# Two-layer attention and experts kernel: 72 tiles of layer 0 made always, five behind a branch

## The chip, the core and the metric

The kernel runs on one core of a Trainium2 chip. A core has five engines that work at the same time, each from its own list of instructions: PE (matrix products), DVE (element by element work and reductions), ACT (activations and copies), POOL (element work, and the DMAs whose rows are looked up) and SP (DMAs). They wait for each other on semaphores. The metric is the time of one execution in microseconds (us); lower is better. The kernel before takes 2041.83 us, the median of 6 runs that reach from 2031.76 to 2045.89.

## What is computed

The input x is 8 sequences of 1024 tokens of 128 numbers. Two layers follow each other, each an attention and a set of experts, and each part is added to what came in:

```python
x = x + L0_attention(layernorm(x))   # 8 heads of 32, softmax
x = x + L0_experts(layernorm(x))     # 14 experts, each token goes to 2
x = x + L1_attention(layernorm(x))   # linear attention, 16 heads of 8
x = x + L1_experts(layernorm(x))     # 8 experts, each token goes to 1
```

The experts of layer 0 are what the change is about. A gate gives each token 14 logits; the two largest choose its experts and its two weights w. Each expert is a small network, y = gelu(x W1 + b1) W2 + b2 with 256 hidden numbers, and the token's result is x + w0 y0 + w1 y1. So 2 x 8192 = 16384 pairs of a token and an expert are to be worked, and how many fall to which expert is known only when the kernel runs.

## The kernel before

**Layer 0 attention** (up to about 1310 us of the profiled execution) computes the attention, the gate and the choice of experts. Each token's normalised row is copied by a DMA on POOL (line 582, `rows_in<-xn,at`) into a table in DRAM, `rows_in`, which has a region of 256 + 8192 rows for each expert. The first 256 rows of each region, and a spare tile at the end, are zeroed at the start of the kernel from a tile of zeros, `nil` (issued through the helper at line 207, inside `load_rest`); so that an expert's tiles can be filled up with zeros in front.

**Layer 0 tiles.** The rows of an expert are cut into tiles of 256 (`TW0`). An expert with r rows has r / 256 tiles, rounded up; each of 14 experts can waste less than one tile, so at most 16384 / 256 + 13 = 77 tiles (`NT0`) are needed. The kernel always makes 77. `expert_tables` (lines 117 to 158) works out with a few small DVE operations, for each tile j, which expert it belongs to (`exp_j`) and which row of `rows_in` it starts at (`row_j`); `upto` is the running sum of tiles over the experts, and its last entry the number of tiles that hold a row. Tiles past that number take the last expert's weights and the spare tile of zeros. SP and DVE read six entries of the tables at a time into registers (`looked_up`, line 167).

The loop over j (from line 941) is written out in full, and PE, DVE, ACT and SP keep the order in which it is written; POOL's instructions are placed by a scheduler. For each tile:

- SP fetches 256 rows (line 863, `xr<-rows_in`), four tiles ahead.
- DVE copies the expert's weights from the table `blob` to `wt` (line 871), two tiles ahead.
- PE transposes the rows (line 877, `px`), ACT copies them out (line 879, `xt`).
- PE makes the hidden numbers (line 886, `ph`), ACT applies gelu (line 889, `g`).
- PE makes the output (line 896, `py`), DVE adds b2 and the row itself (lines 901 and 905, `y`).
- POOL writes the tile to the table `rows_out` in DRAM (line 906, `rows_out<-y`).

Between the tiles DVE works out where each token's two results stand in `rows_out` (`found`, in `places`). At j = 8 the loads and constants of layer 1 are issued, and at j = NT0 - 8 an unread gather on POOL (`warm`, line 843), which the scheduler has placed ahead of the first write of a tile.

**Layer 1 attention** begins when `rows_out` is whole. POOL gathers for each 128 tokens the rows of their two experts (line 1054, `got<-rows_out,found`), ACT and DVE weigh and add them (lines 1073 and 1079), and the normalisation, products and so on follow from line 1089. The first gather on POOL waits for all writes of `rows_out`, in a row of separate waits.

**Layer 1 tiles** end the kernel in the same way, and there a branch exists already: 36 tiles are made always, a flag `over` is read into a register of each engine (line 1627) and the rest of the tiles stands behind `tc.If(crowd > 0)` (line 1631), which is passed over in the profiled execution. A branch of this kind has no meeting of all engines. Each engine reads the flag itself, compares and jumps. On the path that skips the work, each engine raises the semaphores that the skipped work would have raised, so that waits further on keep their numbers; on POOL that is an instruction of its own, `INC_SWDGE_SEM`.

Of the kernel before, what the change touches and what calls it, by code (L numbers as in the profile page):

```python
# [12 lines left out]
ALU = mybir.AluOpType  # L13
# [3 lines left out]
P = 128  # L17
NB = 8
T = 1024
D = 128  # L20
# [8 lines left out]
E0, F0 = 14, 256  # L29
K0 = F0 // P  # L30
CAP0 = NB * T
TW0 = 256
TI0 = TW0 // P

NT0 = 2 * NB * T // TW0 + E0 - 1
REG0 = TW0 + CAP0
ROWS0 = E0 * REG0 + TW0

# [22 lines left out]
NT1_MAIN = 36  # L61
ROWS1 = E1 * REG0 + TW0
RW1 = 2 * D + 1
# [8 lines left out]
C_J = C_TW + CAP0 // TW0  # L72
C_TOK = C_J + NT0
C_END = C_TOK + NCHUNK
# [3 lines left out]
def tile_two_layers(  # L78
# [5 lines left out]
    nc = tc.nc  # L84
# [96 lines left out]
    rows_in = dram.tile([ROWS0, D], F32, name="rows_in")  # L181
    rows_out = dram.tile([NT0 * TW0, D], F32, name="rows_out")

# [4 lines left out]
    counts = routes.tile([P, E0], F32, name="counts")  # L188
    nc.gpsimd.memset(counts, 0.0)
    found = routes.tile([P, NB, 2, CPB], U32, name="found")  # L190
    layer0w = ctx.enter_context(ExitStack())
    blob = layer0w.enter_context(tc.tile_pool(name="blob", bufs=1)).tile([P, E0, B_END], F32, name="blob")

    with ExitStack() as ph:
# [11 lines left out]
        def pinned(f, *args, **kw):  # L206
            return tc.keep_in_program_order(f(*args, **kw))  # L207
# [17 lines left out]
        def load_rest():  # L225
            for b in range(1, NB):
                pinned(nc.sync.dma_start, out=xs[b], in_=x[b].rearrange("(c p) d -> p c d", p=P))
            pinned(nc.sync.dma_start, out=blob, in_=blob0)
            nil = work.tile([P, TI0 * D], F32, name="nil", tag="nums", bufs=1)
            pinned(nc.gpsimd.memset, nil, 0.0)  # L230
            pinned(
                nc.gpsimd.dma_start,
                out=rows_in[:E0 * REG0, :].rearrange("(e r) d -> e r d", e=E0)[:, :TW0, :].rearrange(
                    "e (p i) d -> p e (i d)", i=TI0
                ),
                in_=nil.unsqueeze(1).to_broadcast([P, E0, TI0 * D]),
            )
            pinned(
                nc.gpsimd.dma_start,
                out=rows_in[E0 * REG0:, :].rearrange("(p i) d -> p (i d)", i=TI0), in_=nil,  # L240
            )

        vs, outs = {}, {}
# [467 lines left out]
        for n, qb in blocks:  # L711
            for kc in range(CPB):
                for hp in range(2):
# [30 lines left out]
                    if hp == 1:  # L744
                        weighing = (n, qb, kc, e)
                        if kc % 2 == 0:
                            first = e
# [98 lines left out]

    with ExitStack() as ph:
        tab = ph.enter_context(tc.tile_pool(name="b_tab", bufs=1, reuse_waits="tile"))  # L850
        work = ph.enter_context(tc.tile_pool(name="b_work", bufs=2, reuse_waits="tile"))
        px = ph.enter_context(tc.tile_pool(name="b_px", bufs=2, space=PSUM, reuse_waits="tile"))
        ph_ps = ph.enter_context(tc.tile_pool(name="b_ph", bufs=4, space=PSUM, reuse_waits="tile"))
        py_ps = ph.enter_context(tc.tile_pool(name="b_py", bufs=2, space=PSUM, reuse_waits="tile"))

        tables0 = expert_tables(tab, px, "px", counts, E0, NT0)
        row_of = looked_up(tables0.row_j, NT0, mybir.EngineType.SP, E0 * REG0)
        expert_of = looked_up(tables0.exp_j, NT0, mybir.EngineType.DVE, E0 - 1)

        def fetch(j):  # L860
            r = row_of(j)
            t = work.tile([P, TI0, D], F32, name="xr", bufs=6)
            nc.sync.dma_start(
                out=t, in_=rows_in[bass.ds(r, TW0), :].rearrange("(p i) d -> p i d", i=TI0)
            )
            return t

        def stage(j):
            e = expert_of(j)
            t = work.tile([P, 1, B_END], F32, name="wt", bufs=4)  # L870
            nc.vector.tensor_copy(t, blob[:, bass.ds(e, 1), :])
            return t[:, 0, :]

        def turn(t):
            ps = px.tile([P, TI0, P], F32, name="px")
            for i in range(TI0):
                nc.tensor.transpose(ps[:, i, :], t[:, i, :], ident)  # L877
            xt = work.tile([P, TW0], F32, name="xt", bufs=3)
            nc.scalar.copy(xt, ps.rearrange("p i t -> p (i t)"))
            return xt  # L880

        def hidden0(w, xt):
            g = work.tile([P, K0, TW0], F32, name="g", bufs=3)
            for k in range(K0):
                ps = ph_ps.tile([P, TW0], F32, name="ph")
                nc.tensor.matmul(  # L886
                    ps, lhsT=w[:, B_W1 + k * P:B_W1 + (k + 1) * P], rhs=xt, start=True, stop=True
                )
                nc.scalar.activation(g[:, k, :], ps, AF.Gelu, bias=w[:, B_B1 + k:B_B1 + k + 1])
            return g  # L890

        def output0(j, t, w, g):
            ps = py_ps.tile([P, TI0, D], F32, name="py")
            for i in range(TI0):
                for k in range(K0):
                    nc.tensor.matmul(  # L896
                        ps[:, i, :], lhsT=g[:, k, i * P:(i + 1) * P],
                        rhs=w[:, B_W2 + k * D:B_W2 + (k + 1) * D], start=k == 0, stop=k == K0 - 1,
                    )
            y = work.tile([P, TI0, D], F32, name="y", bufs=4)  # L900
            nc.vector.tensor_tensor(
                y, ps, w[:, B_B2:B_B2 + D].unsqueeze(1).to_broadcast([P, TI0, D]), ALU.add
            )

            nc.vector.tensor_tensor(y, y, t, ALU.add)  # L905
            nc.gpsimd.dma_start(  # L906
                out=rows_out[j * TW0:(j + 1) * TW0, :].rearrange("(p i) d -> p i d", i=TI0), in_=y
            )

        def places():  # L910

            half = NB // 2 * CPB
            shape = [P, half, E0]
            for b in range(0, NB, NB // 2):
                for k in range(2):
                    bs = slice(b, b + NB // 2)
                    pick = work.tile(shape, F32, name="pick", bufs=1)
                    of_expert = chosen[:, k, bs, :].rearrange("p b c -> p (b c)").unsqueeze(2).to_broadcast(shape)
                    yield lambda: nc.vector.tensor_tensor(
                        pick, of_expert, cst[:, C_I14:C_I14 + E0].unsqueeze(1).to_broadcast(shape), ALU.is_equal  # L920
                    )
                    yield lambda: nc.vector.tensor_tensor(
                        pick, pick, tables0.base.unsqueeze(1).to_broadcast(shape), ALU.mult
                    )
                    to = work.tile([P, half], F32, name="to", bufs=1)
                    yield lambda: nc.vector.tensor_reduce(to, pick, AX.X, ALU.add)
                    yield lambda: nc.vector.tensor_tensor(
                        found[:, bs, k, :], ranks[:, k, bs, :], to.rearrange("p (b c) -> p b c", b=NB // 2),
                        ALU.subtract,
                    )  # L930

        with tc.manual_schedule(
            engines={
                mybir.EngineType.PE, mybir.EngineType.DVE, mybir.EngineType.Activation, mybir.EngineType.SP
            }
        ):
            placing = places()
            made, ahead = [], [fetch(j) for j in range(4)]
            weights = [stage(j) for j in range(2)]
            t = ahead.pop(0)  # L940
            ready = [(t, turn(t))]
            for j in range(NT0):
                if j + 4 < NT0:
                    ahead.append(fetch(j + 4))
                if j + 2 < NT0:
                    weights.append(stage(j + 2))
                if ahead:
                    t = ahead.pop(0)
                    ready.append((t, turn(t)))
                (t, xt), w = ready.pop(0), weights.pop(0)  # L950
                made.append((j, t, w, hidden0(w, xt)))
                if len(made) > 1:
                    output0(*made.pop(0))
                if j == 8:
                    load_layer1()
                    make_layer1()
                if j == NT0 - 8:
                    warm()
                if j >= 16 and j % 3 == 1:
                    for piece in placing:  # L960
                        piece()
                        break
            output0(*made.pop(0))
            assert next(placing, None) is None
    layer0w.close()


# [8 lines left out]
    with ExitStack() as ph:  # L976
# [504 lines left out]
        p = NPAIR - 1  # L1481
# [15 lines left out]
        first, second = (Route(NB - 1, c0, CPB // 2) for c0 in (0, CPB // 2))  # L1497
# [28 lines left out]
    with ExitStack() as ph:  # L1526
        tab = ph.enter_context(tc.tile_pool(name="d_tab", bufs=1, reuse_waits="tile"))
# [97 lines left out]
        with ExitStack() as main:  # L1625
            tiles1(main, 0, NT1_MAIN)
        crowd = nc.values_load(
            over, min_val=0, max_val=NB * T,
            skip_runtime_bounds_check_because="it is made of counts",
# [199 lines left out]
```

## Time and profile before

| what | value |
|---|---|
| median of 6 runs | 2041.83 us (2031.76 to 2045.89) |
| the profiled execution: time | 2046.37 us |
| the profiled execution: span from first to last instruction | 2044.6 us |
| mean granted clock of PE | 0.955 |
| PE busy | 1936.1 us (95%) |
| DVE, ACT, POOL busy | 1393.2, 1114.7, 1206.0 us |
| layer 0 tiles | from 1322.5 us (first fetch) to 1480.9 us (last write issued) |
| first gather of layer 1 | 1487.0 us |

The page gives busy times by engine, 40 slices of the span, DMA queues, shares of the chain that ended last, and the costliest groups of instructions. Four views of the trace are used beside it: the chain of what ended last in order of time, where each step is followed back to what released it, and "issue" is time in which an engine waited for nothing that is shown; windows, which give the busy time of each engine and the granted clock of PE in stretches of time; the instructions of one line, with the entries of an engine's sequencer marked by a q (POOLq, DVEq); and the timeline. PEld is the loading of weights into PE, which overlaps its products. A tile's name stands to the left of the arrow where it is written and to the right where it is read.

### The profile page before, as it was taken

The numbers are of one execution on the slowest core, as the hardware profiler recorded it, in microseconds if no ns is written. First come the engines' busy times: TensorE is split into PE (matmuls) and PEld (weight loads), VectorE is DVE, ScalarE is ACT, GpSimd is POOL, SyncE is SP. The second block draws the span as 40 slices with busy tenths as digits, with TensorE's granted clock in tenths as the row PEclk, the third lists the DMA queues.
The fourth block names the chain that finished last, engine by engine and source line by source line (L and its number), as shares of the span: only waits on it lengthen the run. The fifth ranks groups of instructions, "written<-read, shape, count | busy, mean of one in ns | idle before, by whom it ended". The sixth has DMA issues, their size and how long they took to land. (4 is left out here: it accounts for less than half of the span.)

```text
span 2044.6 us, 45296 instructions
## 1 busy us (share of the span) xinstructions
PE 1936.1 (95%) x17406; PEld 1003.6 (49%) x17406; DVE 1393.2 (68%) x3565; ACT 1114.7 (55%) x2351; POOL 1206.0 (59%) x1320
## 2 busy tenths in 40 slices
PE   7999999999999999999999997499959999996997
PEld 3333333333333333333333333299837777775897
DVE  6667768768768768768767776566637777775453
ACT  2555665665565565565555454266536666762443
POOL 1456556667667766766766766422255467644465
PEclk9899999999999999999999998699959999996999
DMA  7000000000000000000000000144322211111331
GB/s 228 1 2 2 2 2 3 8 8 8 9 8 8 9 6 9 8 8 9 8 8 8 13 8 26 36 133 135 124 60 74 88 60 54 49 37 62 107 108 58
DMA packets 49807, 81.58 MB, mean 40 GB/s; under 512 B 13369, under 2 KB 32384, under 8 KB 49456
## 3 DMA queue, kind: packets, MB, share of 16 engines
q0 software_dynamic: 17808, 41.55, 6.0%
q1 hardware_dynamic: 28384, 29.10, 4.9%
q10 hardware_dynamic: 3392, 7.95, 1.2%
q8 instruction: 140, 2.29, 0.5%
q14 instruction: 83, 0.68, 0.1%
HBM read 42.73 MB, written 35.96 MB: 38 GB/s over the span
## 5 line engine op out<-in xcount | busy, mean ns | idle before, releaser
L338 DVE TENSOR_REDUCE nmp<-big 128x1 f32<-128x512 f32 x1000 | 642.2, 683 | 289.0 <-PE st L374 245.9
L377 ACT ACTIVATE e<-st 128x512 f32<-128x512 f32 x1000 | 544.5, 595 | 480.8 <-PE st L374 423.6
L207 POOL TENSOR_TENSOR e<-e 128x512 f32<-128x512 f32 x488 | 604.0, 1268 | 53.2 <-PE num L391 52.7
L334 PE MATMUL big<-kT,qT 32*128 32x512 f32 x2000 | 633.2, 645 | 0.2 <-DVE nmp L338 0.2
L374 PE MATMUL st<-qT,kT 32*128 32x512 f32 x2000 | 535.0, 592 | 0.0
L391 PE MATMUL num<-e,v 128*32 128x512 f32 x3064 | 302.7, 469 | 8.5 <-ACT nums L419 8.5
L207 POOL TENSOR_TENSOR outT<-nums,dens 128x64 f32<-128x64 f32 x248 | 80.7, 326 | 353.3 <-DVE dens L409 259.2
L374 PEld LDWEIGHTS st<-qT,kT 32*128 32x128 f32 x2000 | 215.2, 192 | 3.7 <-issue 1.7
L373 PE MATMUL st<-nb,ones_h 3*128 3x512 bf16 x1000 | 212.9, 386 | 1.3 <-DVE nmp L338 1.3
L391 PEld LDWEIGHTS num<-e,v 128*32 128x32 f32 x3064 | 61.2, 108 | 298.3 <-issue 271.3
L334 PEld LDWEIGHTS big<-kT,qT 32*128 32x128 f32 x2000 | 194.7, 184 | 22.0 <-DVE nmp L338 17.3
L373 PEld LDWEIGHTS <-ones_h 3*128 3x128 bf16 x1024 | 51.2, 91 | 314.4 <-issue 307.7
L1054 POOL DMA_INDIRECT got<-rows_out,found x128 | 126.3, 987 | 94.3 <-PE tp L1089 43.3
L582 POOL DMA_INDIRECT rows_in<-xn,at x128 | 131.6, 1028 | 38.5 <-issue 29.6
L409 DVE RECIPROCAL dens<-dens 128x64 f32<-128x64 f32 x248 | 130.2, 537 | 17.5 <-ACT dens L404 17.4
L391 PE MATMUL den<-e,ones 128*32 128x512 f32 x1032 | 140.0, 611 | 0.2 <-POOL e L207 0.2
L1599 POOL DMA_INDIRECT out_x<-y,to x72 | 79.1, 1099 | 68.6 <-DVE y L1597 51.8
L1580 ACT ACTIVATE g<-ph,wt 128x256 f32<-128x256 f32 x144 | 63.9, 475 | 86.7 <-PE ph L1577 86.6
L906 POOL DMA_DIRECT2D rows_out<-y x77 | 44.7, 580 | 107.0 <-DVE y L905 99.8
L1109 ACT ACTIVATE qm<-qk,cst 128x256 f32<-128x256 f32 x128 | 54.6, 496 | 53.9 <-DVE qk L1106 53.9
L896 PEld LDWEIGHTS py<-wt,g 128*128 128x128 f32 x616 | 81.0, 192 | 4.0
L896 PE MATMUL py<-wt,g 128*128 128x128 f32 x616 | 81.1, 275 | 0.0
(284 smaller groups left out, 2938.1 us busy)
## 6 DMA issues: line engine op xcount, KB each, us to landing
xr<-rows_in SPq DMA_DIRECT2D x77, 128.0 KB
rows_out<-y POOLq DMA_DIRECT2D x77, 128.0 KB, 2.3
xr<-rows SPq DMA_DIRECT2D x36, 257.0 KB
nb<-part SPq DMA_DIRECT2D x384, 1.0 KB
blob<-in_blob ACTq DMA_DIRECT2D x8, 578.0 KB
blob<-in_blob SPq DMA_DIRECT2D x1, 4494.0 KB
x<-in_x SPq DMA_DIRECT2D x8, 512.0 KB
rows<-nil ACTq DMA_DIRECT2D x9, 257.0 KB
```

The lines of the kernel that those rows point to most:

```text
L207: return tc.keep_in_program_order(f(*args, **kw))
L334: nc.tensor.matmul(ps, lhsT=qTs[n][r, qc * P:(qc + 1) * P], rhs=kTs[n][r, kb * BLK:(kb + 1) * BLK], start=True, stop=True,)
L338: nc.vector.tensor_reduce(nmps[n][:, h, qc, kb:kb + 1], ps, AX.X, ALU.max, negate=True)
L373: nc.tensor.matmul(st, lhsT=ones_h[r3, :], rhs=nbs[n][r3, cols], start=True, stop=False)
L374: nc.tensor.matmul(st, lhsT=kTs[n][r, kc * P:(kc + 1) * P], rhs=qTs[n][r, cols], start=False, stop=True)
L377: nc.scalar.activation(e[:, h, :], st, AF.Exp, scale=SCALE0)
L391: nc.tensor.matmul(vds[key][32 * h:32 * h + 32, cols], lhsT=ones[:, :HD0] if den else vs[b][:, kc, c0:c0 + HD0], rhs=e[:, h, cols], start= ...
L409: nc.vector.reciprocal(s[:, cols], s[:, cols])
L582: ins = nc.gpsimd.indirect_dma_start(out=rows_in, out_offset=bass.IndirectOffsetOnAxis(ap=ats[k][:, j:j + 1], axis=0), in_=xn[:, c0 + j, : ...
L896: nc.tensor.matmul(ps[:, i, :], lhsT=g[:, k, i * P:(i + 1) * P], rhs=w[:, B_W2 + k * D:B_W2 + (k + 1) * D], start=k == 0, stop=k == K0 - 1,)
L1054: ins = tc.keep_in_program_order(nc.gpsimd.indirect_dma_start(out=gots[p][:, i, k, :], out_offset=None, in_=rows_out, in_offset=bass.Indir ...
L1599: ins = nc.gpsimd.indirect_dma_start(out=out_rows, out_offset=bass.IndirectOffsetOnAxis(ap=at[:, i:i + 1], axis=0), in_=y[:, i, :], in_off ...
```

## The change

The loop over tiles becomes a function, `tiles0(ph, first, last)`, which is called twice: for tiles 0 to 71, and, behind a branch, for tiles 72 to 76. The flag `over0` is the number of tiles that hold a row, less 72, and at least 0; it is made by one DVE operation right behind the tables. The tables are made once, for 77 tiles, and kept in a pool that now outlives the loop. The work that is woven into the loop (`places`, layer 1's loads, `warm`) stays in the first call. The five last tiles' rows of `rows_out` are zeroed at the start of the kernel, by one more DMA on POOL behind the two that zero rows of `rows_in`. In the built program, the bodies behind the branch hold 52 instructions of PE, 32 of DVE, 20 of ACT, 17 of SP and 11 of POOL; the order of all other instructions is as before but for two neighbours in the tables.

```diff
+NT0_MAIN = 72
...
+            pinned(
+                nc.gpsimd.dma_start,
+                out=rows_out[NT0_MAIN * TW0:, :].rearrange("(j p i) d -> p j (i d)", p=P, i=TI0),
+                in_=nil.unsqueeze(1).to_broadcast([P, NT0 - NT0_MAIN, TI0 * D]),
+            )
...
-    with ExitStack() as ph:
-        tab = ph.enter_context(tc.tile_pool(name="b_tab", bufs=1, reuse_waits="tile"))
+    tab0 = layer0w.enter_context(tc.tile_pool(name="b_tab", bufs=1, reuse_waits="tile"))
+    over0 = tab0.tile([1, 1], mybir.dt.int32, name="over0")
+    held0 = SimpleNamespace()
+
+    def tiles0(ph, first, last):
+
         work = ph.enter_context(tc.tile_pool(name="b_work", bufs=2, reuse_waits="tile"))
...
-        tables0 = expert_tables(tab, px, "px", counts, E0, NT0)
+        if first == 0:
+            held0.tables = expert_tables(tab0, px, "px", counts, E0, NT0)
+            nc.vector.tensor_scalar(
+                over0, held0.tables.upto[0:1, E0 - 1:], float(-NT0_MAIN), 0.0, ALU.add, ALU.max
+            )
+        tables0 = held0.tables
...
-            placing = places()
-            made, ahead = [], [fetch(j) for j in range(4)]
-            weights = [stage(j) for j in range(2)]
+            placing = places() if first == 0 else iter(())
+            made, ahead = [], [fetch(j) for j in range(first, min(first + 4, last))]
+            weights = [stage(j) for j in range(first, first + 2)]
             t = ahead.pop(0)
             ready = [(t, turn(t))]
-            for j in range(NT0):
-                if j + 4 < NT0:
+            for j in range(first, last):
+                if j + 4 < last:
                     ahead.append(fetch(j + 4))
-                if j + 2 < NT0:
+                if j + 2 < last:
                     weights.append(stage(j + 2))
...
-                if j == NT0 - 8:
+                if j == NT0_MAIN - 8:
                     warm()
...
+    with ExitStack() as ph:
+        tiles0(ph, 0, NT0_MAIN)
+    crowd0 = nc.values_load(
+        over0, min_val=0, max_val=NT0, skip_runtime_bounds_check_because="it is made of counts",
+    )
+    with tc.If(crowd0 > 0):
+        with ExitStack() as ph:
+            tiles0(ph, NT0_MAIN, NT0)
     layer0w.close()
```

## The prediction

> **What bounds the kernel now.** I read the page first. PE is busy 95% of the span, so a tile of layer 0 that is left out is worth what it costs on PE, if PE sets the pace in that stage. The view of windows says that it does: in seven stretches of 20 us from 1332 to 1472 us PE is busy for 20.00 of 20.00 with the granted clock at 1.00, while DVE is at 13 to 15, ACT at 13 and POOL at 6. Then I read the chain of what ended last, at the end of the tiles. Its columns are start, duration and what ran, in us:
>
> ```profile
> 1472.21 0.89 PE py L896 x8
> 1473.10 0.22 PE px L877 x2
> 1473.32 0.86 PE ph L886 x4
> 1474.19 0.89 PE py L896 x8
> ...
> 1477.92 1.80 PE py L896 x16
> 1479.74 0.44 DVE y L901
> 1480.20 0.44 DVE y L905
> ...
> 1480.92 1.98 DMA rows_out<-y
> ...
> 1483.65 3.30 issue
> 1486.96 1.00 POOL got L1054
> ```
>
> One tile is px, ph and py on PE, and nothing stands between them: the step from py to py is 0.89 + 0.22 + 0.86 = 1.97 us. (From 1331.99 to 1365.56 the same chain has 17 steps, 33.57 / 17 = 1.975 us.) Behind the last tile the chain leaves PE: the last y, its write to rows_out (1.98 us to landing), POOL's waits, 3.30 us in which POOL waits for nothing that is shown, then the first gather of layer 1. PE stands still from 1479.7 to 1498.3. So whatever the branch adds to POOL behind the last write is paid in full; what it adds to the other four engines has some 10 us of cover.
>
> For the price of a branch the kernel has one of its own, at its end, also passed over. The view of lines 1627 (reading the flag) and 1631 (the branch) gives each engine's sequencer; the columns are count, least/median/greatest duration in ns, and the first and last start in us:
>
> ```profile
> L1627 POOLq TENSOR_LOAD <-over x1: 498/498/498, 2033.0 to 2033.0; - x1
> ...
> L1631 POOLq EVENT_SEMAPHORE  x4: 17/43/43, 2036.4 to 2037.3; - x4
> L1631 DVEq EVENT_SEMAPHORE  x2: 21/21/21, 2035.4 to 2035.5; - x2
> ...
> L1631 ACTq COMPARE_BRANCH  x1: 58/58/58, 2028.5 to 2028.5; - x1
> L1631 ACTq EVENT_SEMAPHORE  x1: 17/17/17, 2029.0 to 2029.0; - x1
> L1631 PEldq COMPARE_BRANCH  x1: 3615/3615/3615, 2029.9 to 2029.9; - x1
> L1631 DVEq COMPARE_BRANCH  x1: 72/72/72, 2032.4 to 2032.4; - x1
> L1631 POOLq COMPARE_BRANCH  x1: 53/53/53, 2033.6 to 2033.6; - x1
> ...
> L1631 POOLq INC_SWDGE_SEM  x1: 1380/1380/1380, 2037.4 to 2037.4; - x1
> ```
>
> The reader is to see how far each engine jumps. By the built program the skipped body there holds 100 instructions of ACT, 295 of DVE, 246 of POOL and 482 of PE. ACT is past its jump 0.5 us after the branch began (2028.5 to 2029.0). DVE needs 3.0 us, POOL 2.8, and PE's branch itself 3.6. A short jump is cheap, a long one costs about 3 us.
>
> **The change, part by part.**
>
> *Tiles left out.* Whether the branch is passed over depends on the data. The reference's own routing on its inputs gives the 14 experts 1020 to 1447 rows (1020, 1119, 1116, 1288, 1304, 1077, 1447, 1061, 1116, 1063, 1138, 1369, 1012, 1254); rounded up to tiles of 256 that is 4+5+5+6+6+5+6+5+5+5+5+6+4+5 = 72. The flag is max(72 - 72, 0) = 0, so the five tiles are skipped. Per tile go 8 matmuls and their weight loads, a copy of weights and two adds on DVE, 3 instructions on ACT, a fetch on SP and a write on POOL. By the chain only PE's counts: 5 x 1.975 = **9.9 us saved**. The fill and drain of the tile pipeline are the same as before, one stage earlier.
>
> *Zeroing five tiles of rows_out.* One more write on POOL at about 12.3 us, 5 x 128 KB. The same write of 14 tiles takes POOL 1.33 us and that of one 0.61, so this takes about 0.8 us; POOL next has work at 59.9 us. The 0.66 MB on the DMA engines are some 1.9 us at the 352 GB/s of the window 30 to 35 us. All loads are through by 35 us (the window 35 to 40 shows 5 GB/s), and SP's next transfers leave at 44.2. Cost 0. Without that cover it would be 1.9 us.
>
> *The flag.* One small DVE operation in the tables (their neighbours of this kind take 0.15 to 0.24 us), and the lists of instructions show no other move than two neighbours changing places. row_j is ready at 1319.8; reading it takes SP 0.5 to 1.5 us, so 1321.3 at the latest, and the first fetch leaves at 1322.5, behind the scatter into rows_in that lands at 1322.3. Cost 0 with about 1 us of cover, 0.2 us without.
>
> *The branch on PE, ACT, DVE and SP.* Reading the flag (0.28 to 0.49 us) and jumping over 52, 20, 32 and 17 instructions, all shorter than ACT's 100. ACT and DVE next work on the first gather, nearly 10 us after their last tile, PE at 1498.3. Cost 0; even a jump of 3.6 us would be covered.
>
> *The branch on POOL.* Here all is on the path. Measured from the start of the last write's issue: now the write lands at 2.0, the ten waits are through at 2.7, the first gather starts at 6.0 (1480.92, 1482.92, 1483.61, 1486.96). With the branch, in the sequencer's order: reading the flag 0.1 to 0.6, the branch and a jump of 11 instructions to about 1.1 (ACT's 0.5 us), two waits to 1.2, then the semaphore update that stands in for the skipped writes, 1.38 us, to 2.55. The write's 2.0 us of landing lie beside this. Twelve waits follow, of which the first is for that update; the eleven others come at 0.085 us each: 3.5 instead of 2.7. Then the same 3.30 us gap. That is **0.8 us added**. Queued behind it on POOL are the gathers, and ACT, DVE and PE wait for those. Bounds: 0, if the update overlaps the landing; 0.8 + 2.8 = 3.6, if the jump costs what POOL's cost at the end; and 0.8 + 4.9 = 5.7, if the update keeps POOL busy as long as the 4.9 us drain that follows it at the kernel's end. Below nothing: the 3.30 us gap is unexplained; if POOL's own work closes it, up to 3.3 us are gained. I take 0.8, by the rows nearest in distance.
>
> [...]
>
> *PE's clock.* The windows behind the gap (PE, PEld, DVE, ACT, POOL busy, then the granted clock):
>
> ```profile
> 1500.00:1525.00 25.00, 18.01 (x140) 10.10 (x143) 12.47 (x43) 12.88 (x33) 14.11 (x16) 0.50 0.23 67
> 1525.00:1550.00 25.00, 25.00 (x339) 17.32 (x332) 13.44 (x48) 12.49 (x31) 13.78 (x15) 0.74 0.28 76
> ```
>
> The clock stays at half until about 1538 while PE is already full. The half-clock spells of this trace come in multiples of 3.41 us (54.6 here, 17.1 at 53 us, 34.1 at 1296). The stage moves by 9.1 us, which is 2.7 such steps, so this spell may end two or three steps earlier: plus or minus one step, worth half of 3.41, 1.7 us. I count it as 0.
>
> [...]
>
> **Sum:** -9.9 + 0.8 = -9.1 us. The profiled execution took 2046.37 us (span 2044.6 and 1.8 around it), which gives 2037.3. The runs shown have their median at 2041.83, 4.5 below it, so I forecast 2041.83 - 9.1 = **2032.7 us**, or 0.45% less. About 0.5% (10.2 us) is what a measurement of this kernel can tell from no change.
>
> **The rivals.**
> - *The jump stalls POOL.* For it: all three long jumps took 2.8 to 3.6 us. Against it: 11 instructions here, ACT's 100 passed in 0.5, and POOL's 2.8 may hold a wait for its last writes. It gives 2032.7 + 2.8 = 2035.5.
> - *The unexplained gap gives way.* If the 3.30 us run from the last write and not from the last wait, the branch is free (2031.9); if the update wakes POOL, up to 3.3 more go (2029.4). Against it: the update is no gather.
> - *Slower: PE's half clock lasts longer.* The first work behind the gap is thin (18.01 of 25), and if it misses the point at which the clock returns, every further 3.41 us cost 1.7. From six such steps on (10.2 us) the gain is gone; at eight, 2032.7 + 13.6 = 2046.3. For it: 54.6 us of half clock stand there already. Against it: the work behind the gap is the same.
> - *The change doesn't skip.* If one expert passed a tile's edge (the nearest has 1020 of 1024), the five tiles would be made in a second round: from the first fetch at 1322.5 to the first y at 1330.9 are 8.4 us, four more tiles 7.9, the branch 0.8: 17.1 instead of 9.9, so 2049.
>
> **How the numbers follow.** Forecast 0.76; the stall 0.12; the gap 0.06; the longer half clock 0.04; no skip 0.02. The range takes the bounds of POOL's part (-3.3 to +4.9), the clock's 1.7 and some 3 us by which a median moves when single runs reach from 2031.8 to 2045.9: 2026 to 2041. The forecast lies 1.1 us short of 0.5%, less than that scatter, so about two fifths of its chance counts as faster, and most of the gap's: 0.35. The last two rivals end within 0.5% at the sizes given and pass it only with scatter on top: 0.02 for slower. Within 0.5%: 0.63.
>
> **What would show it.** The step from py to py stays 1.975 us and the last is the 72nd; the first gather starts 6.9 us after the start of the last write; POOL's branch shows a fraction of a us to its next record, and 1.4 us of update; PE's idle gap is 18.6 + 0.8 us. Wrong would be a gap on POOL over 9 us, records inside the branch, or a half-clock spell of another length.

## The result and the profile after

The changed kernel takes **2031.72 us** (median of 17 runs, 2020.6 to 2036.77), the kernel before, run beside it, 2039.64 us (median of 38). The ratio is 0.9956, with a 95% interval of 0.9941 to 0.9971: 9.0 us less, between 5.9 and 12.0. The forecast was 2032.7 us, 9.1 us less, or 0.45%; the measured ratio is 0.44% less.

The chain of what ended last, at the end of layer 0's tiles (start, duration, what ran):

```profile
1450.77 15.99 DMA rows_out<-y
1467.67 0.19 DVE row L1091
1467.86 3.29 issue
1471.15 1.00 POOL got L1078
```

The first line is no single write: the last one landed at 1465.35. What raised its semaphore at 1466.8 is the end of POOL's semaphore update (shown below), which stands in for the skipped writes. So the chain leaves PE and runs through the update, and crosses a DVE copy that waits for the same semaphores. Then the 3.3 us of "issue" stand ahead of the first gather, as before. The last write starts at 1463.30, so the gather comes 7.85 us behind it; before it was 6.04, and the forecast was 6.9.

What lies between is in the entries of the sequencers for the reading of the flag (L983) and for the branch (L986):

```profile
L983 POOLq TENSOR_LOAD <-over x1: 652/652/652, 1463.3 to 1463.3; - x1
```

```profile
L986 DVEq EVENT_SEMAPHORE  x2: 21/21/21, 1463.2 to 1463.3; - x2
L986 POOLq EVENT_SEMAPHORE  x2: 43/43/43, 1464.2 to 1464.3; - x2
...
L986 ACTq COMPARE_BRANCH  x1: 54/54/54, 1460.9 to 1460.9; - x1
L986 ACTq EVENT_SEMAPHORE  x1: 17/17/17, 1461.1 to 1461.1; - x1
L986 PEldq COMPARE_BRANCH  x1: 390/390/390, 1461.5 to 1461.5; - x1
...
L986 DVEq COMPARE_BRANCH  x1: 72/72/72, 1463.0 to 1463.0; - x1
L986 POOLq COMPARE_BRANCH  x1: 53/53/53, 1464.0 to 1464.0; - x1
L986 POOLq INC_SWDGE_SEM  x1: 2462/2462/2462, 1464.4 to 1464.4; - x1
```

Every jump is short: ACT, DVE and POOL are at their next record 0.2 us after the branch began, PE's branch takes 0.39. There are no products in the branch; 72 writes stand in the trace. But the last line is not as forecast: the update takes 2.46 us and not 1.38.

The windows (PE, PEld, DVE, ACT, POOL busy, then the granted clock), one among the tiles and two of the same length as those shown of before, from the first product behind the gap on (those of before start 1.7 us behind its first product):

```profile
1440.00:1460.00 20.00, 20.00 (x142) 18.92 (x141) 12.51 (x32) 12.71 (x31) 5.42 (x10) 1.00 0.36 122
1482.50:1507.50 25.00, 15.62 (x143) 9.08 (x147) 12.81 (x43) 13.90 (x36) 15.51 (x17) 0.64 0.25 69
1507.50:1532.50 25.00, 25.00 (x338) 17.30 (x329) 13.42 (x49) 12.49 (x31) 13.77 (x15) 0.74 0.29 76
```

PE is full at full clock to the last tile, and the clock is at half again behind the gap, for 30.7 and 17.1 us where it was 54.6 in one piece.

The two profiled executions differ by more than the medians, 2044.6 to 2027.0 us of span, 17.6. By landmarks:

| stretch | before | after | difference |
|---|---|---|---|
| start to first fetch of layer 0's tiles | 1322.50 | 1314.34 | -8.17 |
| first fetch to first write | 9.62 | 10.04 | +0.42 |
| first write to last write | 148.80 | 138.92 | -9.88 |
| last write to first gather | 6.04 | 7.85 | +1.81 |
| first gather to first fetch of layer 1's tiles | 403.62 | 401.63 | -1.98 |
| from there to the end | 154.00 | 154.25 | +0.24 |

The first row is not the change: two kernels below, e3 and e4, have the same code up to that point, and their first fetches stand 8.3 us apart (1327.99 and 1319.65). The second is not either: the same kernels run again show 8.47 and 8.58 us there. In the last two rows executions differ by more than these figures (layer 1's attention by up to 17 us below). What belongs to the change is -9.88 + 1.81 = -8.07 us.

### The profile page after: what moved, and what is told of

It is laid out like the page before. It is cut to its first block, busy times and chain, and to the rows that moved or that the text cites. A ratio compares the mean times of both kernels' runs of the same rounds, so it can differ in the third digit from the quotient of the medians.

```text
span 2027.0 us, 45100 instructions
## 1 busy us (share of the span) xinstructions
PE 1917.1 (95%) x17336; PEld 991.7 (49%) x17336; DVE 1386.9 (68%) x3551; ACT 1107.6 (55%) x2336; POOL 1203.2 (59%) x1316
## 5 line engine op out<-in xcount | busy, mean ns | idle before, releaser
L415 DVE RECIPROCAL dens<-dens 128x64 f32<-128x64 f32 x248 | 130.2, 537 | 17.1 <-ACT dens L410 17.0
L1383 POOL DMA_INDIRECT rows<-row,where x64 | 63.5, 991 | 29.1 <-issue 12.7
L911 PEld LDWEIGHTS py<-wt,g 128*128 128x128 f32 x576 | 76.1, 193 | 3.8
```

The lines of the kernel that those rows point to most:

```text
L415: nc.vector.reciprocal(s[:, cols], s[:, cols])
```

## The experiments

They ran on three other chips (e1 to e4 and e11 on one, the two repeats, e5 and e6 on a second, e8 to e10 on a third), each beside the kernel before, which takes 2083.7 to 2085.1 us there (medians); the extra time is mostly in layer 1's attention. The stretch from the first write to the first gather is the same there to 0.01 us (154.84 before, 146.78 after), and the small terms are read from it. The ratios, with intervals of about plus or minus 4 to 6 us, can hardly tell 2 us: that of e10 leaves out even the 8.06 us that its trace shows. Layer 1's attention took 433 to 450 us in the profiled executions on those chips, and 450 in e10's, which can hide such a gain; that it did is not shown.

| kernel | first to last write | last write to gather | sum against before | ratio to before |
|---|---|---|---|---|
| before, again | 148.80 | 6.04 | 0 | one run |
| after, again | 138.92 | 7.85 | -8.07 | 0.9971 (0.9948 to 0.9993) |
| e1 72 tiles, no branch | 138.92 | 3.17 | -12.75 | 0.9963 (0.9942 to 0.9985) |
| e2 zeroing alone | 148.80 | 3.00 | -3.04 | 1.0008 (0.9987 to 1.0029) |
| e3 branch's writes on SP | 138.92 | 6.33 | -9.59 | 0.9960 (0.9941 to 0.9978) |
| e4 last two writes on SP | 138.65 | 2.69 | -13.50 | 0.9925 (0.9897 to 0.9954) |
| e5 unread gather late | 138.92 | 7.86 | -8.06 | 0.9980 (0.9956 to 1.0003) |
| e6 ten skipped writes | 138.92 | 9.20 | -6.72 | 0.9978 (0.9952 to 1.0003) |
| e8 all late writes on SP | 138.65 | 3.56 | -12.63 | 0.9952 (0.9933 to 0.9972) |
| e9 two branches | 138.92 | 10.47 | -5.45 | one run |
| e10 zeroing in two | 138.92 | 7.86 | -8.06 | 0.9997 (0.9976 to 1.0018) |
| e11 zeroing twice | 138.92 | 4.87 | -11.05 | 0.9942 (0.9918 to 0.9967) |

Two things were to be explained: the update's 2.46 us, and the 3.3 us ahead of the gather. The first theory for the update (A): it waits until POOL's own writes under way have landed, and takes some 1.4 us from there; in the changed kernel it ends 1.48 us after the last landing. The rival (B): it takes 2.46 us at this place, whatever is under way.

**e1: 72 tiles, no branch.** The loop ends at 72, `rows_out` has 72 tiles, no zeroing (tiles 72 to 76, which hold no rows here, are left out altogether).

```diff
...
-            for j in range(NT0):
+            for j in range(NT0_MAIN):
...
```

> The kernel before with its loop ended at tile 72: no branch, no flag, no zeroing; tiles 72 to 76, which hold no rows with these inputs, are left out for good. It prices the skipped tiles alone. Both theories: 5 x 1.975 = 9.9 us less than before, and the first gather 6.0 us after the start of the last write, as before. If instead the tiles were worth only the 7.9 us that the change gained, the branch would be free and the gain of this kernel would be 7.9 too.

The tiles are worth what was forecast, 9.88 us (148.80 less 138.92). But the gather came 3.17 us after the last write and not 6.0. POOL's timeline there (start, duration, what ran, idle time before it):

```profile
1472.10 0.54 POOL L907 DMA_DIRECT2D rows_out<-y  x1 [0.36 <-DVE y L906]
1475.27 0.99 POOL L1055 DMA_INDIRECT got<-rows_out,found  x1 [2.63 <-issue]
```

POOL's last wait ended at 1474.54, so the gap ahead of the gather was 0.72 us and not 3.30, which nothing here had called for.

**e2: the zeroing alone,** in the kernel before.

```diff
+            pinned(
+                nc.gpsimd.dma_start,
+                out=rows_out[NT0_MAIN * TW0:, :].rearrange("(j p i) d -> p j (i d)", p=P, i=TI0),
+                in_=nil.unsqueeze(1).to_broadcast([P, NT0 - NT0_MAIN, TI0 * D]),
+            )
```

> The kernel before with the zeroing of the last five tiles' rows at the start and nothing else; all 77 tiles are made. Theory: 0 us, since POOL has nothing to do until 59.9 us and the loads are through by 36.9 us at the latest. Rival, that the transfer delays the first loads: up to 1.9 us more.

The ratio, 1.0008 (0.9987 to 1.0029), can't tell the 0 of the forecast from the rival's 1.9 us. The traces say more: the loads are delayed as the rival has it, since the last of SP's first loads ends at 36.8 us here and at 35.3 in e1, which has no zeroing (36.8 in after, 35.5 in before). But the first fetch of layer 0's tiles stands at 1323.27 us in e2 and at 1323.25 in e1, so no cost of it is seen there. And the 3.3 us are gone from the gather here too.

**e3: the writes behind the branch on SP's queue,** so that POOL skips no write and needs no update.

```diff
-            nc.gpsimd.dma_start(
+            (nc.sync if j >= NT0_MAIN else nc.gpsimd).dma_start(
```

> The changed kernel, with the writes of the five tiles behind the branch issued by SP in place of POOL, so that POOL's skipping path holds no semaphore update. Theory (the 1.8 us that the branch adds on POOL are the update): first gather 6.0 us after the start of the last write, 9.9 us less than before, 1.8 less than the changed kernel. Rival (they are the reading of the flag and the jump): still 7.8 us, 8.1 less than before.

Without the update POOL's stretch is 6.33 us, 0.29 over the kernel before: that is what the flag, the branch and its waits add to the path. The other 1.52 of the 1.81 us are the update.

**e4: the last two always-made writes on SP's queue.**

```diff
-            nc.gpsimd.dma_start(
+            (nc.sync if NT0_MAIN - 2 <= j < NT0_MAIN else nc.gpsimd).dma_start(
```

> The changed kernel, with the writes of tiles 70 and 71 issued by SP; the update stays on POOL, but POOL's own last write is that of tile 69, some 3 us earlier. Theory A (the update waits until POOL's own writes have landed and then takes 1.4 to 1.5 us): the update starts when the write of tile 69 has been issued and ends 1.5 us after that one landed, so ahead of the landing of the last write; first gather about 6 us after the start of the last write, 9.9 us less than before. Theory B (the update takes 2.5 us here, whatever stands before it): its length stays 2.46 us from its start wherever that is, and ends 2.5 us after a start that has no write in flight.

The update begins two tiles earlier and ends at 1469.13, ahead of the landing of SP's last write at 1469.87: it is hidden whole (2.69 us from the last write to the gather). It again ends 1.34 us after POOL's own last landing, and again takes 2.42 us: both theories hold.

**The two kernels again.** Does the gap of 3.3 us belong to the program or to the execution?

> The kernel before, once more, for the 3.30 us in which POOL waits for nothing that is shown ahead of the first gather. If they belong to the program (where its code lies, what stands in it), they are there again: 6.0 us from the start of the last write's issue to the first gather. If they belong to the one execution, they may be gone: about 3.4 us. The other steps as in the first trace: 158.5 us from the first fetch to the last write, 77 writes.

> The changed kernel, once more. Time against the kernel before: 0.996. The semaphore update on POOL again starts about 1.1 us after the start of the last write and takes 2.4 to 2.5 us (both theories); the gap of 3.3 us before the first gather either stands (7.8 us from the last write to the gather: the gap belongs to the program) or is gone (5.2 us: it belongs to the execution).

To the program: 6.04 and 7.85 us once more, and the same 2.46 us for the update.

**e5: the unread gather late,** pinned with the writes so that it stands ahead of the 65th.

```diff
-        nc.gpsimd.memset(number, 0)
-        nc.gpsimd.indirect_dma_start(
+        pinned(nc.gpsimd.memset, number, 0)
+        pinned(
+            nc.gpsimd.indirect_dma_start,
...
-            nc.gpsimd.dma_start(
+            pinned(
+                nc.gpsimd.dma_start,
```

> The changed kernel with the unread gather that goes ahead of layer 1, and the writes of the tiles, held in program order, so that this gather stands right before the 65th write and not earlier. It tests the 3.3 us before the first gather. If they are a gather's first start after a long pause (something of its own that has to be fetched again), the late unread gather has paid for them: 5.2 us from the last write to the first gather instead of 7.85, and up to 2.6 us (0.13%) less time. If they have nothing to do with gathers, 7.8 us as before.

It stood at 1464.65, and the gap stayed (3.29 us): this is no gather's first start.

**e6: ten skipped writes.** This is the run that tells A from B.

```diff
...
+            if j < NT0_MAIN:
+                nc.gpsimd.dma_start(out=rows, in_=y)
+            else:
+                for i in range(TI0):
+                    nc.gpsimd.dma_start(out=rows[:, i:i + 1, :], in_=y[:, i:i + 1, :])
```

> The changed kernel, with each of the five writes behind the branch cut in two (not run, since the branch is passed over). Ten skipped writes stand on all eight of POOL's DMA semaphores, and not on five of them, so the update on POOL has to wait by its own semaphores until the last write of the 72 tiles has landed, 2.0 us after its start. First theory (the update waits for POOL's writes under way and then takes 1.4 to 1.5 us): the record of the update is 1.3 to 1.5 us long, ends 1.5 us after that landing, and the first gather comes as in the changed kernel, 7.85 us after the last write (5.2 if the 3.3 us gap is not there). Rival (the update takes 2.46 us at this place whatever is under way): its record is 2.4 to 2.5 us, ends 2.5 us after the landing, and the gather comes 1.0 us later. Time 0.996 by both.

POOL's entries for the branch in e6:

```profile
L989 POOLq EVENT_SEMAPHORE  x4: 17/43/1272, 1476.3 to 1477.8; - x4
...
L989 POOLq INC_SWDGE_SEM  x1: 2447/2447/2447, 1477.9 to 1477.9; - x1
```

The wait of 1.27 us holds POOL until the last write has landed (1477.63); only then does the update begin, and it still takes 2.45 us. **Theory A falls.** The update waits for no landing.

**e8: all late writes on SP's queue,** e3 and e4 together.

```diff
-            nc.gpsimd.dma_start(
+            (nc.gpsimd if j < NT0_MAIN - 2 else nc.sync).dma_start(
```

> The changed kernel, with the writes of its last two always-made tiles and of the five tiles behind the branch on SP's queue and no longer on POOL's, so that POOL has no write to stand in for and no semaphore update. POOL runs 202 DMAs of its own before the first gather. Reading of the runs so far: the 3.3 us before the first gather appear where POOL has run 204 or 208 DMAs by then (multiples of four: five kernels) and not at 202, 203 and 209 (three kernels); so 0.7 us of gap here. From the last write to the first gather: 2.0 to landing, 0.9 for waits, 0.7: 2.7 to 3.6 us, instead of 7.85. That is 4.3 to 5.2 us less than the changed kernel, and 12 to 14 us less than the kernel before: ratio 0.993 to 0.994. If the update had cost nothing that its end shows, it would stay at the changed kernel's 0.996.

3.56 us to the gather, as forecast, and 12.6 us less by the trace. The ratio says 10 us less (5.8 to 14): the forecast 12 to 14 lies in its interval, but its middle falls short of it.

**e9: two branches,** tiles 72 to 74 behind one and 75 and 76 behind the other (the expectation counts tiles from 1); the zeroing in five writes.

```diff
-            tiles0(ph, NT0_MAIN, NT0)
+            tiles0(ph, NT0_MAIN, NT0_MAIN + 3)
+    with tc.If(crowd0 > 3):
+        with ExitStack() as ph:
+            tiles0(ph, NT0_MAIN + 3, NT0)
```

> The changed kernel, with two branches one after the other (tiles 73 to 75, tiles 76 and 77, both passed over), so that two semaphore updates stand one behind the other on POOL; and the zeroing as five writes of one tile each, so that POOL has run 208 DMAs by the first gather. What fell before: the update took 2.45 us even where the last write had landed before it began, so it waits for no write. Theory now: the update's 2.46 us hold about 1.1 us that only its first run pays (it is at 1.28 to 1.48 us at the kernel's end, its second run): the second update here takes 1.3 to 1.5 us. Rival: 2.46 us is its price at this place each time: the second takes 2.4 to 2.5 as well. And at 208 DMAs, a multiple of four, the gap before the first gather is 3.3 us; if it goes by something else, it may be 0.7.

The two updates, one line from each branch's entries:

```profile
L987 POOLq INC_SWDGE_SEM  x1: 2445/2445/2445, 1467.7 to 1467.7; - x1
```

```profile
L990 POOLq INC_SWDGE_SEM  x1: 2429/2429/2429, 1470.4 to 1470.4; - x1
```

The second costs as much as the first, so it is no price of a first run either. The gap was 3.3 us at 208 DMAs, as the count would have it.

**e10: the zeroing in two writes.**

```diff
+            for a, b in ((NT0_MAIN, NT0_MAIN + 2), (NT0_MAIN + 2, NT0)):
...
```

> The changed kernel, with the zeroing of the five tiles at the beginning done by two writes (two tiles, three tiles) and not by one: 205 DMAs on POOL before the first gather instead of 204. If the 3.3 us before that gather go by this count (multiples of four), the gap falls to 0.7 us and the first gather comes 5.25 us after the start of the last write instead of 7.85, 2.6 us less time than the changed kernel: ratio to the kernel before 0.994 to 0.995. If the gap belongs to the branch or to the update, it stays: 7.85. The update on POOL again takes 2.46 us.

The gap stayed at 205 DMAs: **the rule of multiples of four falls.** What took its place came from looking where the 2.58 us (3.30 less 0.72) had gone in the kernels without the gap. In e2 they stand ahead of the fifth write from the end; its chain of what ended last (start, duration, what ran):

```profile
1471.54 0.54 POOL rows_out L912
1472.07 1.42 issue
1473.51 0.54 POOL rows_out L912
1474.05 4.00 issue
1478.07 0.50 POOL rows_out L912
```

Between two writes there are 1.42 us; here 4.00, though this tile's y was ready in time: 2.58 more. In e4 a part of them stands ahead of the third gather:

```profile
1470.86 1.00 POOL got L1078
1471.86 0.31 issue
1472.16 0.98 POOL got L1078
1473.15 1.19 issue
1474.34 0.95 POOL got L1078
```

e2 puts five tiles of rows more on POOL's queue, and the stall comes five DMAs earlier; e4 puts two tiles less there, and it comes two DMAs later. So it stands behind a fixed amount of DMA work.

**e11: the zeroing twice,** to move the stall on purpose.

```diff
+            for _ in range(2):
+                pinned(
+                    nc.gpsimd.dma_start,
...
```

> The changed kernel, with the zeroing of the five tiles done twice at the beginning, one write after the other: 206 DMAs on POOL before the first gather, and five tiles' worth of rows more than the changed kernel. Reading of the runs so far: POOL's DMA work stalls once for 2.58 us behind a fixed number of rows that POOL has moved. In both kernels that is right ahead of the first gather, since the zeroing of five tiles stands for the five writes left out; five tiles more put it five writes earlier. So the fifth write from the end (tile 68 of 72) should start about 2.9 us after its y and not 0.3, the gap before the first gather should fall from 3.3 to 0.7 us, and the first gather come 5.25 us after the start of the last write instead of 7.85: 2.6 us less than the changed kernel. Rival: the stall belongs to the first gather behind a branch or to an update and stays there: 7.85. The update takes 2.46 us by both. Time against the kernel before: 0.994 to 0.995 by the first, 0.996 by the second; the time alone will hardly tell them apart.

POOL's timeline at the last writes:

```profile
1466.49 0.54 POOL L922 DMA_DIRECT2D rows_out<-y  x1 [1.44 <-DVE y L921]
1471.05 1.69 POOL L922 DMA_DIRECT2D rows_out<-y  x3 [4.01 <-DVE y L921]
```

The fourth write from the end (tile 68, counted from 0) started 2.88 us after its y, where 0.3 is usual, and the gap ahead of the gather was 0.72 us. The stall went where it was sent, one write beside the forecast. POOL issued 205 DMAs ahead of the first gather, not the 206 of the expectation, and so as many as in e10, which has the gap: what counts is not how many DMAs there are but what they hold. The update's entry in e11 had been forecast at 2.46:

```profile
L987 POOLq INC_SWDGE_SEM  x1: 426/426/426, 1475.4 to 1475.4; - x1
```

Right behind the stall, the update takes 0.43 us, at the same place in the program: **theory B falls too.** The gather came 4.87 us after the start of the last write, 0.4 less than forecast. Of the 2.0 us that the update saved, 1.65 went to the writes bunched behind the stall: POOL waited 1.20 us for their landings ahead of the update and 0.44 behind it, until the last had landed, 3.15 us after its start. A stall that moves, and an update that is cheap right behind it, suggest what both are.

**One reading for both.** The stall comes back. Behind the first gather, POOL's DMAs of layer 1 show a long step (3.1 to 4.0 us where 1.55 or 2.2 is usual) at number 212 (the first gather is 0) in before, after, their repeats, e3, e5, e6, e9 and e10, 207 in e2, 208 in e11, 214 in e4 and e8, 217 in e1. Each time it is 212 DMAs behind the place of the first stall (in e1, which shows none, ahead of the sixth gather, where five tiles less would put it). POOL's timeline there, in after and in e2 (start, duration, line, idle time before it):

```profile
1921.73 0.98 POOL L1623 DMA_INDIRECT out_x<-y,to  x1 [0.30 <-issue]
1925.43 0.98 POOL L1623 DMA_INDIRECT out_x<-y,to  x1 [2.72 <-DVE to L1616]
```

```profile
1956.69 1.25 POOL L1605 DMA_INDIRECT out_x<-y,to  x1 [1.20 <-DVE y L1603]
1960.10 1.57 POOL L1605 DMA_INDIRECT out_x<-y,to  x1 [2.16 <-issue]
```

For after the profile names DVE's `to`, but that is the next tile's; this DMA's own y ended at 1923.68, and its like start 0.3 us behind their y or the DMA before them. Of the 72 DMAs at that line this one alone is later than that by more than 0.3 us, by 1.5 to 1.9 us, in all fourteen traces.

Halfway, 106 DMAs behind the stall, six traces show a smaller late step: number 108 in e4 and e8 (1.61 and 2.36 us, elsewhere 1.32), 111 in e1 (1.58), 102 in e11 (1.62), 101 in e2 (3.13, elsewhere 1.95), 106 in e10 (1.88, elsewhere 1.26). The other eight show none there, nor does before 106 DMAs ahead of its first stall, where POOL's steps are 1.26 to 1.28 us. So 212 is what the traces show; that something fills up after 106 DMAs of the size of a gather or a tile's write is a reading of them. By it the update's time goes by how far it has filled. POOL runs 264 DMAs from the first gather to the update at the kernel's end:

| update | DMAs since the last filling | measured | 0.35 + 0.020 for each |
|---|---|---|---|
| e11, at the branch | 4 | 0.43 | 0.43 |
| e1, at the end | 264 - 5 - 212 = 47 | 1.28 | 1.29 |
| before and after, at the end | 264 - 212 = 52 | 1.38, 1.36 | 1.39 |
| e2, at the end | 264 + 5 - 212 = 57 | 1.48 | 1.49 |
| e11, at the end | 264 + 4 - 212 = 56 | 1.43 | 1.47 |
| e4 and e8, at the end | 264 - 2 - 212 = 50 | 1.32, 1.34 | 1.35 |
| e4, at the branch | 106 - 2 = 104 | 2.42 | 2.43 |
| after, at the branch | 106 | 2.46 | 2.47 |

The line was drawn through these rows after the runs, and no run was made to test it; its two last rows count from a filling 106 DMAs back that no trace shows at that place. The places of the stall were tested by e11.

What it is that fills up is not shown. By the places of the stall in before, after and e11 the zeroing of five tiles counts for more than four tile writes and less than five. Neither its bytes (those of five writes) nor the packets that the trace counts on POOL's queue fit: a tile's write has 48 (240 fewer in e1 than in before, 17568 against 17808, for five writes), the zeroing 176 (17984 in e2), 176 / 48 = 3.7 writes.

## Why the prediction was right

*The tiles left out:* 9.9 us forecast, 9.88 measured, in every kernel with 72 tiles whose writes all go through POOL.

*The zeroing, the flag, the branch on PE, ACT, DVE and SP:* costed at 0. No time for the zeroing is seen in e2, and PE is full to the last tile. The prediction did not see what the zeroing does: it puts on POOL's queue about what the five writes take off it (by the places of the stall in before, after and e11, more than four tile writes and less than five), and so the stall stays ahead of the first gather. Without it, in e1, the 3.3 us fell to 0.7. **The prediction's rival that the gap gives way** named a gain of up to 3.3 us; the gap can give way, by 2.58, but to neither of the two reasons given there.

*The branch on POOL:* 0.8 forecast, 1.81 measured. The flag, the branch and the jump were as forecast: the update starts 1.07 us after the last write (1.2 forecast). The short jumps held: 0.2 us on POOL, so the rival of the stalled jump falls. One of the prediction's three long jumps was no measure of a jump, though: POOL's 2.8 us at the kernel's end hold two DMAs of 0.98 us, and POOL is past that branch in 0.75 us in e8 and 1.03 in e1. That a long jump costs about 3 us rests on PE's 3.6 and DVE's 3.0 alone. That the landing lies beside the update held too (1465.35 lies within 1464.37 to 1466.83). **The term that was mis-sized is the update: 1.38 us taken from the kernel's end, 2.46 measured.** The two places are not alike: at the end POOL is 52 DMAs behind a stall, at the branch right ahead of one. That this sets the price is argued from the table above; e11 alone moved the stall and saw the update change with it. The wait was as forecast too: 1.02 us for twelve waits (0.94), then the same 3.3 us. PE's gap grew from 18.60 to 20.42 us, by the same 1.82.

*PE's clock:* counted as 0, plus or minus 1.7. The half-clock spell was shorter by two steps of 3.41 us (47.8 us in two pieces where it was 54.6), and the stage by 2.0 us. A spell of another length was among the prediction's own signs of being wrong. Repeated executions of the two kernels on a second chip show 37.6 and 44.4 us of half clock there, in the opposite order, so the traces give no ground to put it down to the change.

*The sum:* -9.9 + 0.8 = -9.1 forecast; -9.88 + 1.81 = -8.07 by the trace; -9.0 (-12.0 to -5.9) by the runs. The 1.0 us that the update cost more is within that scatter, so that the runs meet the forecast to 0.1 us is luck; the trace is the better test, and it shows one term off by a factor of two. The level was 2.2 us too high as well: before's median was 2041.83 over the 6 runs shown and 2039.64 over 38. And the range, 2026 to 2041, is a little narrower than the plain sum of the parts that it names (2024.7 to 2042.3). The time of the taken branch, the prediction's last rival, was not tried.

A version that is better by the trace is e4 or e8: 13.5 and 12.6 us off the path where the changed kernel takes off 8.07, and 0.9925 (0.9897 to 0.9954) and 0.9952 (0.9933 to 0.9972) in ratio. The intervals overlap that of the changed kernel (0.9941 to 0.9971, and 0.9948 to 0.9993 when run again), and the three were timed on different chips, so in time the gain over it is likely for e4 and open for e8.

## What to carry to other kernels

A duration taken from another place of the same trace holds only if that instruction's price doesn't depend on where it stands (the update took 1.38 us at the kernel's end and 2.46 at the branch); ask what differs between the two places, and take both ends where that isn't known. Before you cost a branch on POOL, look at what POOL owes for the DMAs that it skips: writes moved to another engine's queue take the update away or put it beside other work (last write to gather: 6.33 us in e3, 2.69 in e4 and 3.56 in e8, where the changed kernel has 7.85). A gap that no view explains is best moved on purpose: a harmless DMA more, as in e11, where the gap fell from 3.30 to 0.72 us, shows whether it belongs to the instruction behind it or to what has run before. And before you take the time from a branch to the next record as the price of its jump, look for work of that engine that falls into it (two DMAs of 0.98 us in POOL's 2.8 us here).

## What the runs showed of the hardware

- POOL's DMA work stalled for up to 2.58 us in these runs, at places set by the DMA work that went before, and not by the instruction that stands there (ahead of the fifth write from the end in e2, of the fourth in e11, of the first gather in e10); the next one came 212 DMAs later (a start 1.5 to 1.9 us late). Beside PE's work it cost nothing in e2 (148.80 us from the first write to the last, as in before), in e11 the writes that bunch behind it cost 1.65 us, and ahead of the first gather it was paid in full (a gap of 3.30 us in before, 0.72 in e1). Why e4 shows 0.9 us of it ahead of the third gather and e1 none ahead of the sixth stays open.
- The semaphore update that stands in for skipped DMAs on POOL took 0.43 (e11) to 2.46 us (after). It went neither by how many writes were skipped (2.46 us for five, 2.45 for ten) nor by whether the last write had landed (2.45 us in e6, begun behind the landing, 2.46 in after, begun ahead of it); its place between two stalls fits its times in the table above.
- A skipped body of 11 to 52 instructions cost an engine 0.2 us (POOL, ACT, DVE in after) to 0.7 us (PE in e4); at the kernel's end one of 295 cost DVE 3.0 and one of 482 cost PE 3.6 (before).
